# Four adjacency chunks issued first, weights on GpSimd's queue, and row sums turned by transposes, in a four-layer graph network

## The chip, the cores and the metric

The kernel runs on one core of one Trainium2 chip. The metric is the device time of a run in microseconds. A core has five engines: TensorE (PE, with its weight loads shown apart as PEld), VectorE (DVE), ScalarE (ACT), GpSimd (POOL) and SyncE (SP). SP, ACT and POOL issue DMA transfers here.

## The reference

The input is x (2708 nodes by 128 features) and a matrix adj (2708 by 2708, float32). Four graph layers follow each other, each on a normalised copy of x and each added to x. Cut to what matters here:

```python
def _lap_mul(A, x):                       # layer 0, used twice
    d = 1.0 / jnp.sqrt(jnp.sum(A, axis=-1))
    return d[:, None] * (A @ (d[:, None] * x))

h = jnp.maximum(_layernorm(x), 0.0)
z = leaky_relu(_lap_mul(adj, h) @ W1 + b1, 0.1)
S = exp(-distance(z, z) / 2), with all but the 4 largest of each row set to 0
x = x + _lap_mul(S + adj, h) @ W2 + b2
...
x = x + attention_layer(relu(layernorm(x)), adj)          # layer 1
x = x + h @ W_self + (adj @ h / max(rowsum(adj), 1)) @ W_neigh   # layer 2
x = x + relu((adj @ h) @ kernel + bias)                    # layer 3
```

The row sums of adj (the degrees) are needed before the first product with adj can be made, because its other factor is h scaled by one over their root.

## The kernel before, in words

adj goes in transposed, so a row of what the kernel loads is a column of adj. It is cut into T = 22 chunks of 128 rows (the last has 20), each 128 by 2708 float32, or 1354 KB. A chunk is used in six column blocks, KBS, five of 512 and one of 148 columns. The nodes are kept as 22 tiles of 128, in six GROUPS of four.

`chunk(i)` (line 242 for its load) issues a chunk's load on SP's queue. The last five chunks of the first pass have places of their own (`res`); the others share the pool `big` of four buffers, so the load of chunk i + 4 waits until the work on chunk i is done. The completion of loads issued by SP and ACT is counted on eight semaphores that are handed out in turn; a load whose semaphore is still in use waits for the load that uses it. POOL's loads have eight others.

The start, in program order:

- Constants (the identity by POOL), then the loads of x (lines 85 and 86), of six weights (line 90), three biases (95), the attention vector (105) and the store of a constant to `order_d` (137), all on ACT's queue.
- `layernorm_relu` for the six groups (lines 171 to 181): statistics on DVE, a root on ACT, and 22 scaled rows h0 on ACT.
- The first pass over adj: for each chunk, six products with a matrix of ones (line 341) add up the row sums in two PSUM tiles, four column blocks of the first tile and two of the second lying in bands of 32 partitions. Between the chunks `weighted(g, part)` is put, one part per chunk from chunk 3 on and kept at its place in PE's order: part 0 transposes four tiles of h0 (line 309) and ACT copies them to h0T (314), part 1 multiplies by W1 (line 320, copied to y1 by ACT, line 327), part 2 by W2 (copied to hw2 by DVE).
- The sums go to SBUF (`sum_rows`), and 44 instructions of TensorE, two for each tile (22 products), multiply one row of 128 sums by a one (line 358), which puts them into columns; seven copies put these into `degs`. From it come `rdeg` and `dinv`, and y1 is scaled (line 191).
- The first aggregation (line 255), which goes over adj again from its first chunk, with `to_z` at its end.

`evacuate` (lines 149 and 151) copies from PSUM to SBUF with DVE and ACT in turn, over all its calls in the kernel; its state is one bit. After the aggregation come the distances and the four nearest nodes (lines 448 to 480), a gather of rows (524), the second aggregation, layer 1 with sorting, a table and gathers of its rows (lines 587 to 1126), and two more aggregations for layers 2 and 3. In each aggregation the products of one chunk are made for all column blocks, and the chunks kept in SBUF come last, block by block, while `done` finishes the block before.

The order of instructions on each engine is set when the program is built, by priorities and by what is marked with `pin`, which keeps it in program order.

Of the kernel before, what the change touches and what calls it, by code (L numbers as in the profile page):

```python
# [9 lines left out]
F32 = mybir.dt.float32  # L10
# [8 lines left out]
P = 128  # L19
# [6 lines left out]
def kernel(  # L26
# [18 lines left out]
    nc = tc.nc  # L45
    N, D = x.shape
    assert D == P
    T = -(-N // P)
    TAIL = N - (T - 1) * P
    KBS = [(k0, min(512, N - k0)) for k0 in range(0, N, 512)]  # L50
    NKB = len(KBS)
    GROUPS = [(t, min(t + 4, T)) for t in range(0, T, 4)]
    L0_RES = 5
    TAIL_RES = 6

    def width(t):
        return TAIL if t == T - 1 else P

    def cols(t):
        return slice(t * P, t * P + width(t))  # L60
# [7 lines left out]
    big = ctx.enter_context(tc.tile_pool(name="big", bufs=4))  # L68
    dram = ctx.enter_context(tc.tile_pool(name="dram", bufs=1, space=DRAM))
    ps_s = ctx.enter_context(tc.tile_pool(name="ps_s", bufs=2, space=PSUM))  # L70
    ps_a = ctx.enter_context(tc.tile_pool(name="ps_a", bufs=1, space=PSUM))


    ident = consts.tile([P, P], F32, name="ident")
    make_identity(nc, ident)
    ones = consts.tile([P, P], F32, name="ones")
# [10 lines left out]

    def load_w(name, w):
        t = consts.tile([P, P], F32, name=name)
        nc.scalar.dma_start(t, w)  # L90
        return t

    def load_b(name, b):
        t = consts.tile([P, P], F32, name=name)
        nc.scalar.dma_start(t, bass.AP(tensor=b.tensor, offset=b.offset, ap=[[0, P], [1, P]]))
        return t

    w1, w2 = load_w("w1", l0_w1), load_w("w2", l0_w2)
    wg = load_w("wg", l1_w)
    ws, wn = load_w("ws", l2_ws), load_w("wn", l2_wn)  # L100
    w3 = load_w("w3", l3_k)
    b1, b2, b3 = load_b("b1", l0_b1), load_b("b2", l0_b2), load_b("b3", l3_b)
    a_nat = consts.tile([P, 2], F32, name="a_nat")
    with nc.allow_non_contiguous_dma(reason="256 elements"):
        nc.scalar.dma_start(
            a_nat, bass.AP(tensor=l1_a.tensor, offset=l1_a.offset, ap=[[1, P], [P, 2]])
        )
    ident_b = consts.tile([P, P], BF16, name="ident_b")
# [24 lines left out]
    order_d = dram.tile([P * T, 2], F32, name="order_d")  # L133
    nowhere = consts.tile([P, T, 2], F32, name="nowhere")
    nc.vector.memset(nowhere[:, :, 0:1], 1e6)
    nc.vector.memset(nowhere[:, :, 1:2], -1e5)
    nc.scalar.dma_start(order_d.rearrange("(p t) c -> p t c", t=T), nowhere)

    LAST = -(-(N - (T - 1) * PER + 3) // 16) * 16
    HALF = KBS[NKB // 2][0]  # L140
# [5 lines left out]
    def evacuate(dst, src):  # L146
        turn[0] ^= 1
        if turn[0]:
            nc.vector.tensor_copy(dst, src)
        else:  # L150
            nc.scalar.copy(dst, src)

    def pin(ins):

        return tc.keep_in_program_order(ins)

    def acc(b):
        return ps_a.tile([P, 512], F32, name=f"acc{b}")

    def span(g):  # L160
        return slice(GROUPS[g][0] * P, min(GROUPS[g][1] * P, N))
# [36 lines left out]
    def inv_sqrt(name, v):  # L198
        r = small.tile([P, T], F32, name=name + "_s")
        nc.scalar.activation(r, v, AF.Sqrt)  # L200
        d = keep.tile([P, T], F32, name=name)
        nc.vector.reciprocal(d, r)
        return d
# [25 lines left out]
        for t in range(t0, t1):  # L229
            use(t, p[: width(t), t - t0, :])  # L230

    resident = {}
    pools = {}

    def chunk(i):
        if i in resident:
            return resident[i]
        if i >= T - pools["n"]:
            c = resident[i] = pools["res"].tile([P, N + 1], F32, name=f"res{i}")
        else:  # L240
            c = big.tile([P, N + 1], F32, name="chunk", tag="big")
        pin(nc.sync.dma_start(c[: width(i), :N], adjT[i * P : i * P + width(i), :]))
        return c

    def aggregate(y, done, more=None, kept=0):

        out = [acc(b) for b in range(NKB)]
        last = T - pools["n"]  # L250

        def product(i, b):
            k0, n = KBS[b]
            w = width(i)
            nc.tensor.matmul(  # L255
                out[b][:, :n],
                y[:w, i, :],
                chunk(i)[:w, k0 : k0 + n],
                start=(i == 0),
                stop=(i == T - 1),  # L260
            )

        for i in range(last):
            if more is not None:
                more(i)
            resident[i] = chunk(i)
            for b in range(NKB):
                product(i, b)
            if i < last - kept:
                del resident[i]  # L270
            if i % 2 and last + i // 2 < T:
                chunk(last + i // 2)
        if more is not None:
            for i in range(last, T):
                more(i)
        for b in range(NKB):
            for i in range(last, T):
                product(i, b)
            if b:
                done(b - 1, out)  # L280
        done(NKB - 1, out)

    NG = len(GROUPS)
    degs = keep.tile([P, T], F32, name="degs")
    nc.vector.memset(degs, 1.0)


    rows_open = ExitStack()
    res_rows = rows_open.enter_context(tc.tile_pool(name="rows", bufs=1))
    pools.update(res=res_rows, n=L0_RES)  # L290
    l0 = ExitStack()
    res = l0.enter_context(tc.tile_pool(name="l0_res", bufs=1))

# [9 lines left out]
    def weighted(g, part):  # L303
        t0, t1 = GROUPS[g]
        if part == 0:
            p = acc(g % 2)
            for t in range(t0, t1):
                o = (t - t0) * P
                mm = nc.tensor.transpose(
                    p[:, o : o + width(t)], h0[: width(t), t, :], ident[: width(t), : width(t)]  # L310
                )
                if t == t0:
                    pin(mm)
            nc.scalar.copy(h0T[:, span(g)], p[:, : span(g).stop - span(g).start])
            return
        dst, w = ((y1, w1), (hw2, w2))[part - 1]
        p = acc(2 * part + g % 2)
        for t in range(t0, t1):
            o = (t - t0) * P
            mm = nc.tensor.matmul(  # L320
                p[: width(t), o : o + P], h0T[:, cols(t)], w, start=True, stop=True
            )
            if t == t0:
                pin(mm)
        for a, e, n in ((t0, min(t1, T - 1), P), (max(t0, T - 1), t1, TAIL)):
            if a < e:
                (nc.scalar.copy, nc.vector.tensor_copy)[part - 1](
                    dst[:n, a:e, :],
                    p[:n, (a - t0) * P : (e - t0) * P].rearrange("p (t f) -> p t f", f=P),
                )  # L330
# [3 lines left out]
    for i in range(T):  # L334
        c = chunk(i)
        w = width(i)
        if 3 <= i < 3 + 3 * NG:
            weighted((i - 3) // 3, i % 3)
        for b, (k0, n) in enumerate(KBS):
            g = 32 * (b % 4)  # L340
            nc.tensor.matmul(
                sums[b // 4][g : g + 32, :n],
                ones[:w, :32],
                c[:w, k0 : k0 + n],
                start=(i == 0),
                stop=(i == T - 1),
            )
    sum_rows = lay.tile([P, 1024], F32, name="sum_rows", tag="U")
    for half, p0, p1 in ((0, 0, 128), (1, 0, 32 * (NKB - 5)), (1, 32 * (NKB - 5), 32 * (NKB - 4))):
        n = KBS[4 * half + p0 // 32][1]  # L350
        evacuate(sum_rows[p0:p1, 512 * half : 512 * half + n], sums[half][p0:p1, :n])

    pd = [acc(j) for j in range(4)]
    for b, (t0, t1) in enumerate(GROUPS):
        j = b % 4
        for t in range(t0, t1):
            o = 512 * (b // 4) + P * (t % 4)
            nc.tensor.matmul(
                pd[j][: width(t), t : t + 1],
                sum_rows[32 * j : 32 * j + 1, o : o + width(t)],  # L360
                ones[32 * j : 32 * j + 1, :1],
                start=True,
                stop=True,
            )
    for b, (t0, t1) in enumerate(GROUPS):
        e = min(t1, T - 1)
        evacuate(degs[:, t0:e], pd[b % 4][:, t0:e])
    evacuate(degs[:TAIL, T - 1 :], pd[(NG - 1) % 4][:TAIL, T - 1 : T])
    dinv = inv_sqrt("dinv", degs)

    nc.gpsimd.tensor_tensor(xs, xs, b2[:, None, :].to_broadcast([P, T, D]), ALU.add)
# [53 lines left out]
    p = ps_s.tile([P, 512], F32, name="ps")  # L425
    pin(nc.tensor.transpose(p[:, :P], wg, ident))
    nc.vector.tensor_copy(wgT, p[:, :P])
    p = ps_s.tile([P, 512], F32, name="ps")
# [14 lines left out]
    for t in range(T):  # L443
        w = width(t)
# [245 lines left out]
    def rowtile(name):  # L690

        i = row_turn[0]
        row_turn[0] = (i + 1) % L0_RES
        return res_rows.tile([P, N + 1], F32, name=name, tag=f"res{T - L0_RES + i}")
# [229 lines left out]
    p = acc(0)  # L924
# [44 lines left out]
    for t0, t1 in GROUPS:  # L969
        p = acc(1 + t0 // 4 % 5)  # L970
        for t in range(t0, t1):
            o = (t - t0) * P
# [4 lines left out]
                start=True,  # L977
                stop=True,
# [3 lines left out]
        for t in range(t0, t1):  # L982
            o = (t - t0) * P
# [31 lines left out]
    for t in range(T):  # L1015
        if t + 3 < T:
            fetch(t + 3)
        o = rowtile("knots")
        for b, (k0, n) in enumerate(EKBS):
            p = acc(b)  # L1020
# [30 lines left out]
    rows, factors = {}, {}  # L1051
# [227 lines left out]
```

## Time and profile before

| | |
|---|---|
| median of 5 runs | 1318.88 us (1310.98 to 1320.64) |
| profiled execution | 1314.6 us, its span 1312.6 us |
| mean granted TensorE clock | 0.901 |
| busy, share of the span | PE 83%, PEld 39%, DVE 43%, ACT 31%, POOL 17% |
| chain that ended last | PE 57%, DMA 17%, DVE 10%, issue 9% |
| DMA | 297 MB, 227 GB/s over the span |
| first sums of chunk 0 | at 7.50 us |
| first product of line 255 | at 95.68 us |

The span is the time from the first to the last instruction. A row of a timeline gives the start, the busy time, the engine, the line, the operation with its tiles, how many there were, and in brackets how long the engine was idle before and what ended that. The rows of a wait view give who waited for whom, the total, how often, and the longest. The rows of a DMA view give a queue's packets, megabytes, and the time of its packets as a share of the 16 DMA engines; q1 is SP's queue, q10 ACT's and q0 POOL's. The granted clock is 1.00 at full speed.

### The profile page before, as it was taken

To read this page: it belongs to the slowest core of one execution; us is meant where nothing else is said; L and a number is where in the kernel's file an instruction comes from. 1 tells how busy PE (TensorE), PEld (TensorE's weight loads), DVE (VectorE), ACT (ScalarE), POOL (GpSimd) and SP (SyncE) were. 2 spreads that over 40 slices of the span, in tenths; PEclk is the share of its full clock that TensorE was granted. 3 is DMA by queue.
4 is the path that set the end of the run, shared out by engine and by line. 5 is a ranking of instruction groups with operands and counts; after the bars stand their busy time and mean duration, and the time that the engine had idled before them with its cause. 6 is when DMAs were issued, how large, how long until landed. Compare 5 with 4: busy or idle time off the path is not lost.

```text
span 1312.6 us, 10207 instructions
## 1 busy us (share of the span) xinstructions
PE 1090.9 (83%) x3637; PEld 514.6 (39%) x3637; DVE 564.1 (43%) x1172; ACT 408.2 (31%) x643; POOL 227.6 (17%) x188
## 2 busy tenths in 40 slices
PE   4879999999683369897776871587889999999998
PEld 1334444444231124464433430233344445545444
DVE  2020026999822001783455763899970031113003
ACT  3100014444400000475666743677840021003000
POOL 0100000000077710034111102576400000000000
PEclk8989999999795579887899986888889999999999
DMA  8997800000463351256799997999949926752831
GB/s 318 424 384 257 292 1 1 0 1 0 171 265 96 94 225 81 87 229 234 213 390 394 368 381 306 422 422 412 354 161 420 352 78 227 267 184 81 302 125 43
DMA packets 39506, 297.31 MB, mean 227 GB/s; under 512 B 6749, under 2 KB 10680, under 8 KB 13116
## 3 DMA queue, kind: packets, MB, share of 16 engines
q1 hardware_dynamic: 23806, 201.04, 40.1%
q0 software_dynamic: 13216, 93.62, 19.0%
q10 hardware_dynamic: 2434, 2.01, 0.6%
q8 instruction: 29, 0.48, 0.1%
q14 instruction: 21, 0.17, 0.0%
HBM read 264.46 MB, written 32.87 MB: 227 GB/s over the span
## 4 chain that ended last, share of the span: by engine, by line
PE 57%; DMA 17%; DVE 10%; issue 9%; another core or an unknown queue 6%; POOL 1%; ACT 1%; SPq 0%; POOLq 0%; DVEq 0%; ACTq 0%
PE acc L255 37%; DMA mov<-in_adj_dram,src_u 8%; PE acc L448 8%; DVE hi L1116 3%; DMA chunk<-in_adj_dram 3%; DVE hi L1104 3%; DMA hi<-table,hi_u 2%; PE acc L454 2%; PE acc L1021 2%; DMA res<-in_adj_dram 2%; PE ps L224 1%; PE acc L1126 1%; DMA xs<-in_x_dram 1%; PE ps L222 1%
## 5 line engine op out<-in xcount | busy, mean ns | idle before, releaser
L255 PE MATMUL acc<-chunk,y 128*128 128x512 f32 (+1 forms) x408 | 178.5, 588 | 73.0 <-issue 55.7
L1126 PE MATMUL acc<-hi,xw 128*128 128x512 f32 (+2 forms) x264 | 119.5, 613 | 60.8 <-DVE hi L1116 60.8
L524 POOL DMA_INDIRECT gath<-ydr,near_u x88 | 83.2, 946 | 408.4 <-DMA ydr<-y 322.1
L255 PE MATMUL acc<-chunk,h 128*128 128x512 f32 (+1 forms) x384 | 148.0, 542 | 0.0
L255 PEld LDWEIGHTS acc<-chunk,y 128*128 128x128 f32 x408 | 78.9, 203 | 172.6 <-issue 158.3
L1021 PE MATMUL acc<-mov,wt 128*128 128x512 f32 (+1 forms) x264 | 114.9, 588 | 35.2 <-DMA mov<-in_adj_dram,src_u 32.7
L448 PE MATMUL acc<-zT 128*128 128x512 f32 (+2 forms) x264 | 107.7, 552 | 0.0
L1126 PEld LDWEIGHTS acc<-hi,xw 128*128 128x128 f32 (+1 forms) x264 | 53.7, 212 | 126.6 <-DVE hi L1116 63.7
L1025 DVE COPY mov<-acc 2x512 f32<-2x512 f32 (+1 forms) x126 | 74.3, 611 | 60.0 <-PE acc L1021 58.3
L255 PEld LDWEIGHTS acc<-chunk,h 128*128 128x128 f32 x384 | 68.8, 190 | 74.1 <-issue 74.1
L1021 PEld LDWEIGHTS acc<-mov,wt 128*128 128x128 f32 x264 | 51.0, 204 | 95.3 <-issue 78.8
L457 ACT COPY strip<-acc 128x512 f32<-128x512 f32 (+2 forms) x132 | 60.5, 559 | 71.4 <-issue 58.5
L255 PE MATMUL acc<-chunk,attended 128*128 128x512 f32 x192 | 73.8, 547 | 0.0
L1058 POOL DMA_INDIRECT lo<-table,lo_u x22 | 56.9, 2585 | 76.3 <-DVE hi L1104 35.3
L448 PEld LDWEIGHTS acc<-zT 128*128 128x128 f32 (+1 forms) x264 | 46.6, 186 | 56.3 <-issue 35.5
L1026 ACT COPY knots<-acc 128x512 f32<-128x512 f32 x88 | 50.2, 585 | 57.2 <-DVE mov L1025 36.5
L1104 DVE SCALAR_TENSOR_TENSOR hi<-lo,lam,hi 128x2708 f32<-128x2708 f32 (+4 forms) x25 | 67.2, 2697 | 1.0
L1116 DVE SCALAR_TENSOR_TENSOR hi<-row_all,inv_s,hi 128x2708 f32<-128x2708 f32 (+4 forms) x25 | 67.0, 2692 | 0.0
L1108 ACT ACTIVATE hi<-hi,lam 128x2708 f32<-128x2708 f32 (+4 forms) x25 | 56.7, 2280 | 32.9 <-issue 23.8
L459 DVE MAX8 top_v<-strip 128x8 f32<-128x2708 f32 (+1 forms) x22 | 64.7, 2966 | 0.5 <-ACT strip L457 0.4
L461 DVE FIND_INDEX8 top_i<-top_v,strip 128x8 uint32<-128x2708 f32 x20 | 59.2, 2974 | 0.0
L255 PE MATMUL acc<-res,h 128*128 128x512 f32 (+1 forms) x144 | 58.9, 551 | 0.0
(267 smaller groups left out, 1162.4 us busy)
## 6 DMA issues: line engine op xcount, KB each, us to landing
chunk<-in_adj_dram SPq DMA_DIRECT2D x110, 1354.0 KB
table<-knots SPq DMA_DIRECT2D x20, 1354.5 KB
res<-in_adj_dram SPq DMA_DIRECT2D x9, 1354.0 KB
ydr<-y SPq DMA_DIRECT2D x2, 704.0 KB
gath<-ydr,near_u POOLq DMA_INDIRECT x88
chunkY<-in_adj_dram SPq DMA_DIRECT2D x1, 1354.0 KB
chunkU<-in_adj_dram SPq DMA_DIRECT2D x1, 1354.0 KB
table<-knots SPq DMA_DIRECT2D x1, 1333.3 KB
```

The lines of the kernel that those rows point to most:

```text
L255: nc.tensor.matmul(out[b][:, :n], y[:w, i, :], chunk(i)[:w, k0 : k0 + n], start=(i == 0), stop=(i == T - 1),)
L448: mm = nc.tensor.matmul(zz[b][:w, :n], zT[:, cols(t)], zT[:, k0 : k0 + n], start=True, stop=False)
L457: nc.scalar.copy(s[:w, k0 : k0 + n], zz[b][:w, :n])
L459: nc.vector.max(top_v[:w, t, :], s[:w, :])
L461: nc.vector.max_index(top_i[:w, t, :], top_v[:w, t, :], s[:w, :])
L524: nc.gpsimd.indirect_dma_start(out=g[:w, :], out_offset=None, in_=ydr[:, :], in_offset=bass.IndirectOffsetOnAxis(ap=near_u[:w, t, k : k + ...
L1021: nc.tensor.matmul(p[:, :n], wt[:, t, :], moving[t][:, k0 : k0 + n], start=True, stop=True)
L1025: nc.vector.tensor_copy(moving[t + 1][:2, k0 : k0 + n], p[:2, :n])
L1058: nc.gpsimd.indirect_dma_start(out=dst[:w, :], out_offset=None, in_=table[:, :], in_offset=bass.IndirectOffsetOnAxis(ap=idx[:w, t : t + 1] ...
L1104: nc.vector.scalar_tensor_tensor(num, lo[:w, c], kap, num, op0=ALU.mult, op1=ALU.add)
L1116: nc.vector.scalar_tensor_tensor(att[:w, c], row_all[:w, c], inv_s[:w, t : t + 1], att[:w, c], op0=ALU.max, op1=ALU.mult,)
L1126: nc.tensor.matmul(py[b][:, :n], xw[:w, t, :], att[:w, k0 : k0 + n], start=(t == 0), stop=(t == T - 1),)
```

## The change

It has two parts. The first four chunks are loaded by calls at the head of the kernel, ahead of the constants, and used when the first pass comes to them; the weights, biases and other small loads move from ACT's queue to POOL's; `weighted` starts at chunk 4 instead of 3. And the row sums are turned into columns by ten transposes, with four copies by DVE, in place of the 22 products and seven calls of `evacuate`. `pin`, `chunk` and the pool `rows` are defined earlier for it, unchanged.

```diff
+    rows_open = ExitStack()
+    res_rows = rows_open.enter_context(tc.tile_pool(name="rows", bufs=1))
+    pools.update(res=res_rows, n=L0_RES)
+    FIRST = 4
+    for i in range(FIRST):
+        resident[i] = chunk(i)
...
     def load_w(name, w):
         t = consts.tile([P, P], F32, name=name)
-        nc.scalar.dma_start(t, w)
+        nc.gpsimd.dma_start(t, w)
         return t
...
-        nc.scalar.dma_start(t, bass.AP(tensor=b.tensor, offset=b.offset, ap=[[0, P], [1, P]]))
+        nc.gpsimd.dma_start(t, bass.AP(tensor=b.tensor, offset=b.offset, ap=[[0, P], [1, P]]))
...
-        nc.scalar.dma_start(
+        nc.gpsimd.dma_start(
             a_nat, bass.AP(tensor=l1_a.tensor, offset=l1_a.offset, ap=[[1, P], [P, 2]])
         )
...
-    nc.scalar.dma_start(order_d.rearrange("(p t) c -> p t c", t=T), nowhere)
+    nc.gpsimd.dma_start(order_d.rearrange("(p t) c -> p t c", t=T), nowhere)
...
-        if 3 <= i < 3 + 3 * NG:
-            weighted((i - 3) // 3, i % 3)
+        if i >= FIRST and i < FIRST + 3 * NG:
+            weighted((i - FIRST) // 3, (i - FIRST) % 3)
...
+        if i < FIRST:
+            del resident[i]
...
-    pd = [acc(j) for j in range(4)]
-    for b, (t0, t1) in enumerate(GROUPS):
-        j = b % 4
-        for t in range(t0, t1):
-            o = 512 * (b // 4) + P * (t % 4)
-            nc.tensor.matmul(
-                pd[j][: width(t), t : t + 1],
-                sum_rows[32 * j : 32 * j + 1, o : o + width(t)],
-                ones[32 * j : 32 * j + 1, :1],
-                start=True,
-                stop=True,
-            )
-    for b, (t0, t1) in enumerate(GROUPS):
-        e = min(t1, T - 1)
-        evacuate(degs[:, t0:e], pd[b % 4][:, t0:e])
-    evacuate(degs[:TAIL, T - 1 :], pd[(NG - 1) % 4][:TAIL, T - 1 : T])
+    for g0, g1 in [(0, 4)] + [(b, b + 1) for b in range(4, NKB)]:
+        pd = acc(max(g0 - 3, 0))
+        r0, r1 = 32 * (g0 % 4), 32 * (g0 % 4 + g1 - g0)
+        e = min(4 * g1, T)
+        for c in range(min(4, e - 4 * g0)):
+            w = min(width(4 * b + c) for b in range(g0, g1))
+            o = 512 * (g0 // 4) + P * c
+            nc.tensor.transpose(
+                pd[:w, P * c : P * c + r1 - r0], sum_rows[r0:r1, o : o + w], ident[r0:r1, r0:r1]
+            )
+        pv = pd.rearrange("p (c g r) -> p g c r", c=4, g=4)[:, : g1 - g0, :, 0]
+        m = min(e, T - 1) - 4 * g0
+        nc.vector.tensor_copy(
+            degs[:, 4 * g0 : 4 * g0 + m].rearrange("p (g c) -> p g c", g=g1 - g0),
+            pv[:, :, : m // (g1 - g0)],
+        )
+        if e == T:
+            nc.vector.tensor_copy(degs[:TAIL, T - 1 :], pd[:TAIL, P * m : P * m + 1])
```

In the built program SP's order is chunks 0 to 3, then chunk 4 (after chunk 0's sums), 5, and 6, which waits for chunk 2's sums and for the semaphore that x's load uses. ACT's order has the two loads of x, the table load, all 22 scaled rows, and then the first copy to h0T. POOL's order has one weight load between the two instructions that make the identity, and the others after them.

More of the change, by code (lines that the diff above doesn't have):

```diff
@@ L71, with pin, chunk @@
     ps_a = ctx.enter_context(tc.tile_pool(name="ps_a", bufs=1, space=PSUM))
+    def pin(ins):
+        return tc.keep_in_program_order(ins)
+    resident = {}
+    pools = {}
+    def chunk(i):
+        if i in resident:
+            return resident[i]
+        if i >= T - pools["n"]:
+            c = resident[i] = pools["res"].tile([P, N + 1], F32, name=f"res{i}")
+        else:
+            c = big.tile([P, N + 1], F32, name="chunk", tag="big")
+        pin(nc.sync.dma_start(c[: width(i), :N], adjT[i * P : i * P + width(i), :]))
+        return c
+    rows_open = ExitStack()
[4 more added lines that the diff above has]
+        resident[i] = chunk(i)
     ident = consts.tile([P, P], F32, name="ident")
@@ L151, in evacuate @@
             nc.scalar.copy(dst, src)
-    def pin(ins):
-        return tc.keep_in_program_order(ins)
     def acc(b):
@@ L230, in node_product @@
             use(t, p[: width(t), t - t0, :])
[L232 to L243, printed above, removed]
     def aggregate(y, done, more=None, kept=0):
@@ L285 @@
     nc.vector.memset(degs, 1.0)
-    rows_open = ExitStack()
-    res_rows = rows_open.enter_context(tc.tile_pool(name="rows", bufs=1))
-    pools.update(res=res_rows, n=L0_RES)
     l0 = ExitStack()
```

## The prediction

> **What bounds the kernel now.** I read the page's chain first: PE has 57% of it and DMA 17%, spread over stages, so a change at the start is worth what it takes off the stretch up to the first product of the first aggregation (line 255). The timeline of that stretch, rows of several engines:
>
> ```profile
> 7.50 3.59 PE L341 MATMUL ps<-chunk,ones 128*32 128x512 f32 x12 [7.50 <-DMA chunk<-in_adj_dram]
> ...
> 15.14 0.49 DVE L171 BATCH_NORM_STATS2 ln_st<-xs 128x6 f32<-128x128 f32 x2 [13.26 <-DMA xs<-in_x_dram]
> ...
> 20.71 3.19 ACT L181 ACTIVATE h<-xs,ln_nm,ln_rs 128x128 f32<-128x128 f32 x8 [0.26 <-DVE ln_nm L176]
> ...
> 27.50 2.98 PE L341 MATMUL ps<-chunk,ones 128*32 128x512 f32 x12 [2.00 <-DMA chunk<-in_adj_dram]
> ...
> 28.46 2.42 ACT L181 ACTIVATE h<-xs,ln_nm,ln_rs 128x128 f32<-128x128 f32 x6
> ...
> 30.41 1.71 PE L320 MATMUL acc<-w,h0T 128*128 128x128 f32 x8
> ...
> 47.44 1.90 PE L341 MATMUL ps<-chunk,ones 128*32 128x512 f32 x12 [0.76 <-DMA chunk<-in_adj_dram]
> ...
> 84.85 3.73 PE L341 MATMUL ps<-res,ones 128*32 128x512 f32 x24 [1.68 <-DMA res<-in_adj_dram]
> ...
> 88.56 4.94 PE L358 MATMUL acc<-ones,sum_rows 1*128 1x1 f32 x44
> ...
> 95.68 16.80 PE L255 MATMUL acc<-chunk,y 128*128 128x512 f32 x38 [2.17 <-DVE y L191]
> ```
>
> The row sums wait for adj from chunk 4 or so to chunk 20 (47.44 is chunk 9, 84.85 chunk 20), one chunk per 3.25 to 3.3 us. From 95.7 on PE runs without a pause for 100 us. So the stretch is a load, a tail of 88.58 to 95.65, and what is lost in front. The loss is in the first 22 us. The waits of the load queue, and then the DMA queues from 5 to 10 us and from 10 to 15 us (packets, MB, share):
>
> ```profile
> SPq L242 <- DMA w<-in_L_gnn_W_dram: 13.6, 1, 13.6
> ```
> ```profile
> q1 hardware_dynamic: 171, 1.67, 82.2%
> q10 hardware_dynamic: 163, 0.33, 17.2%
> ```
> ```profile
> q10 hardware_dynamic: 1115, 1.31, 96.3%
> q1 hardware_dynamic: 18, 0.03, 1.8%
> ```
>
> Two chunks are issued at 0.8 to 1.7 us. The third (15.34) waits 13.6 us on a weight load with whose completion its semaphore is shared. The second pair is the row that decides my forecast: while adj (q1) has work, x (q10) gets one packet of 2 KB for each of adj's, 0.33 MB in 5 us; as soon as adj runs dry, x takes all 16 engines, and lands at 15.14.
>
> **The change, part by part.**
>
> *Chunks 2 and 3 at once.* That ends the waits at 13.6 us and after. But it takes from x the stretch in which it ran alone. The built program issues four chunks, chunk 4 when chunk 0's sums are done (7.5 + 3.6 = 11.1), chunk 5 at about 13.6; chunk 6 waits for the semaphore that x's load uses. So x shares the engines with six chunks. Two ways to its landing: at 0.066 MB/us (the row above) its 21 x 128 x 512 B = 1.38 MB take 20.8 us from the first packet at 5.3, that is 26.1, and the weights' packets and 0.6 us to the semaphore come on top. Or by the sum: six chunks of 1.387 MB, x and 0.6 MB of weights are 10.3 MB; at 400 GB/s (the mean of that view) 25.7 us, from 2.0, plus 0.6: 28.3. Since everything in the queues must be done by then whatever the order, 28.3 is also an upper end. The lower is 24 (x starting 2 us earlier). I take 28.3, 13.2 us later than now.
>
> The Trainium skill, "DMA: Bandwidth & Descriptors", Queues, rings and completion order, says that an engine drains a whole packet of some 9 to 17 descriptors from one queue before it turns to the next. The row shows 9.8 KB, one row of adj, per turn, so the turns here are shorter; by the rule x would get almost nothing until chunk 5 is through, and its landing would still be 28.3, since that is a sum of bytes.
>
> *Layernorm.* ACT loses the eleven issues that held it until 18.64 and its table load after them. In the built program the first scaled rows come after eight statistics pairs at 0.26, a cast, five more statistics at 0.2, two reciprocals and two factors: 4.2 us after x (5.57 now). From the first to the last of the 22 rows ACT takes 10.17 now (20.71 to 30.88), with a copy of 0.56 in it that partly hides; I take 10.1. So they end at 28.3 + 14.3 = 42.6. The copy h0T, which now stands ahead of the last six rows, stands behind all of them in the new order: 43.2. PE, in program order, has the first transposes ahead of chunk 4 (one chunk later than now): 28.3 + 4.2 + 1.6 = 34.1, 0.65 for them, then chunk 4's sums at half clock, 3.6 as at 7.50: 38.4. The first product w1 needs h0T: 43.2, 1.64 (30.41 to 32.05 now), then chunk 5's sums as at 27.50, 2.98: 47.8.
>
> *Four buffers.* Queued behind these PE waits are the releases: chunk 8 goes out at 38.4 and chunk 9 at 47.8. A chunk on an idle queue takes 1.1 us to its first packet (issue at 102.57), 3.3 of transfer and 0.4: chunk 9 lands at 52.6, where it now starts at 47.44: +5.2. PE needs 2.73 a chunk from there (1.90 + 0.83), DMA 3.3, so the rest is load-bound as now and keeps the +5.2. This is the stall that takes the place of the one removed. The last product group now falls between chunks 20 and 21, both landed: +0.8.
>
> *Weights by POOL.* Eleven issues; POOL's gathers take 946 ns each (the group at line 524), so some 10 us, ending near 12. Needed are w1 at 43 and b2 for line 371, which waits for the rows anyway; the identity comes one issue later, needed at 34. Cover: 30 us; without it 1 us per issue. I take nothing. The same page, in Issuing engine by pattern, puts a simple load on SP and calls GpSimd's path the slower one (about 1 us against 0.6 to the first byte); by that the weights would come an estimated 0.4 us later each, under the same cover.
>
> *Ten transposes.* 44 products of one row take 4.94 us, and the degree copies end at 94.01. Instead: the first copy of sums (0.69) as now, four transposes 0.65 (the row of four at line 309), a copy of 0.2, the copy of 148 columns (0.30), the last transposes 0.25 and two copies of 0.16: degrees ready 1.75 us after the last sum where it is 5.4 now. The 1.64 us from there to the first product stay: 3.4 instead of 7.07, -3.65. Bounds: at half clock throughout the transposes cost 0.9 more (-2.75); if the copies overlap fully, -4.2.
>
> *Clock.* The granted clock is 0.50 from 90 to 99.6, so the first 4 us of line 255 run at half: 2.1 us lost. With a shorter pause it may or may not drop: between -2.1 and +1; I take -0.5, nearest to the row as it stands.
>
> *Evacuations.* Seven calls fewer turn the alternation of ACT and DVE round in all later stages (0.57 against 0.69 us for a copy). The two alternate per group, so it is nearly even; -1 to +1, taken as 0.
>
> **Sum.** +5.2 + 0.8 - 3.65 - 0.5 = +1.85 us on the profiled execution: its span of 1312.6 lies in a run of 1314.6, so 1316.5. That run is 4.3 under the median of 1318.88, to which I add the same: 1320.7. About 0.5% (6.6 us) is what a measurement of this kernel can tell from no change, so this is "same". With the bounds (x at 24: -4.3; tail and clock +0.9, +1.5; copies 1) the likeliest case alone runs from 1313 to 1324.
>
> **The rivals.**
>
> *x is not held back (faster).* If x keeps its landing near 15 to 18 us, no PE wait comes, and the load streams throughout: 29.3 + 1.4 + 0.6 = 31.3 MB at 420 GB/s are 74.5 us from 2.0, plus the 1 us that chunk 20 now takes over the usual: 77.5 where it is 84.85, -7.3; with +0.8, -3.65 and -0.5 the sum is -10.7, 1308.2. For it: 11 to 22 us now moves well under 400 GB/s. Against: the 163 against 171 packets. It begins to win over the present load when x lands before 23.
>
> *PE stays cold (slower).* Place: chunks 5 to 9, after two PE pauses of 12 and 5 us. At half clock a chunk takes 3.6 + 1.5 = 5.1 us, over the 3.3 of the load, so each cold chunk from chunk 6 on delays the buffer, and so the load, by 1.8. One or two cold chunks are the 2.98 already in the sum; three bring +5.4, 1326; four 1328. For it: the clock was 0.50 again from 29 to 31 us, right after work had begun at 27.5. Against: from 32 on it was full at 60% duty. The Trainium skill, "TensorE: Matmul & The Clock Gate", Part 1, puts the warm-up at about 3.4 us of sustained work; by that one chunk would be cold and nothing is added, an estimate; the rows of 28 to 32 us are less kind.
>
> *The change does not do what it says.* The first chunk is issued at 0.82 us now, so "ahead of everything" moves only chunks 2 and 3; if x also stays as it is held now, only the transposes are left with their clock, -4.15 and 1314.7, within the same band.
>
> **How the numbers follow.** My case with the last rival has 0.50, faster 0.23, cold PE 0.27. Faster reaches over 0.5% nearly always; cold PE from three chunks on, most of its chance, and my case's edges give 0.04 to slower and 0.01 to faster: 0.24, 0.45, 0.31. The range takes in both rivals: 1307 to 1329.
>
> **What would show it.** Right: statistics (line 192) start near 28, h0T's copy near 43, chunk 9's sums near 52.6, the last sum near 94.6, the first product of line 255 some 3.4 us after it; POOL's issues done by 15. Wrong: statistics before 23, no PE wait on ACT before 45, or granted clock at 0.50 after 48. It would be wrong altogether if stages after 100 us differ in length by over 2 us.

## The result, and the profile after

The changed kernel takes 1324.75 us (median of 42 runs, 1316.35 to 1330.78) where the kernel before takes 1318.46 (79 runs, 1310.55 to 1326.11): ratio 1.0044, 95% interval 1.0032 to 1.0056, or 4.2 to 7.4 us more. The median is under the 0.5% which the prediction set as the bound (the interval reaches 0.56%), but the interval excludes zero, and the loss is larger than the 1.85 us that were worked out. The profiled execution took 1323.66 us with a span of 1321.6 and a mean granted clock of 0.894.

The rows of the changed kernel's timeline that answer to those of the prediction (start, busy time, engine, line, operation, and in brackets the idle time before it and what ended it). Line 192 is the statistics, 202 the scaled rows, 314 the transposes of h0, 319 the copy h0T, 325 the weighted products, 346 the row sums, 368 the ten transposes, 263 the first aggregation:

```profile
30.04 0.49 DVE L192 BATCH_NORM_STATS2 ln_st<-xs 128x6 f32<-128x128 f32 x2 [28.17 <-DMA xs<-in_x_dram]
...
33.73 3.19 ACT L202 ACTIVATE h<-xs,ln_nm,ln_rs 128x128 f32<-128x128 f32 x8 [1.03 <-DVE ln_nm L197]
...
34.36 1.54 PE L314 MATMUL acc<-ident,h 128*128 128x128 f32 x4 [7.11 <-ACT h L202]
...
35.83 3.62 PE L346 MATMUL ps<-chunk,ones 128*32 128x512 f32 x12
...
41.35 2.42 ACT L202 ACTIVATE h<-xs,ln_nm,ln_rs 128x128 f32<-128x128 f32 x6 [0.25 <-DVE ln_nm L197]
...
43.68 0.56 ACT L319 COPY h0T<-acc 128x512 f32<-128x512 f32 x1
...
44.29 2.08 PE L325 MATMUL acc<-w,h0T 128*128 128x128 f32 x8 [4.84 <-ACT h0T L319]
46.30 2.47 PE L346 MATMUL ps<-chunk,ones 128*32 128x512 f32 x12
```
```profile
92.62 1.90 PE L346 MATMUL ps<-res,ones 128*32 128x512 f32 x12 [1.66 <-DMA res<-in_adj_dram]
...
97.08 1.53 PE L368 MATMUL acc<-ident,sum_rows 128*128 128x128 f32 x10
...
100.38 11.87 PE L263 MATMUL acc<-chunk,y 128*128 128x512 f32 x24 [1.77 <-DVE y L212]
```

Read from the top: x lands at 30.0 where it landed at 15.1. PE waits 7.11 us for the first scaled rows, and 4.84 us more for h0T, because ACT makes all 22 rows (33.73 to 43.77) before it turns to the copy. Chunk 20's sums stand at 92.62 (84.85 before). From the last sum to the first product of line 263 it is 3.3 us where it was 7.1. The bottom two rows are the gain, everything above is the loss, and the loss is the larger: the first product starts 4.7 us later.

The waits of the load queue up to 100 us (total, times, longest) show how PE's two waits reach the load. Before, buffers that PE had not released held the queue for 20.4 us, at most 3.1 at a time; now it is 41.3, at most 8.9. The row before, then two rows of the changed kernel:

```profile
SPq L242 <- PE ps L341: 20.4, 10, 3.1
```
```profile
SPq L87 <- PE ps L346: 41.3, 11, 8.9
...
SPq L87 <- DMA xs<-in_x_dram: 13.4, 2, 13.2
```

In the table by stretches (busy time of PE, PEld, DVE, ACT and POOL, each with its count, then granted clock, DMA share, GB/s) the load falls off while PE waits and then works cold (at half the clock):

```profile
35.00:40.00 5.00, 4.45 (x15) 0.93 (x14) 1.88 (x16) 4.75 (x14) 0.00 (x0) 0.50 0.62 259
40.00:45.00 5.00, 0.71 (x3) 0.71 (x4) 0.57 (x4) 3.98 (x11) 1.14 (x1) 0.50 0.79 277
45.00:50.00 5.00, 5.00 (x31) 2.69 (x34) 0.10 (x1) 0.58 (x1) 5.00 (x1) 0.75 0.15 29
```

SP's queue moved nothing from 39.0 to 40.4 and from 45.2 to 49.8. Before, it had one such gap, 11.1 to 16.3. The change traded one gap of 5.2 us for two of 6.0 together, and a load that is slower in front, which the DMA queues from 5 to 10 us show (packets, MB, share):

```profile
q1 hardware_dynamic: 147, 1.42, 73.4%
q10 hardware_dynamic: 130, 0.27, 14.0%
q0 software_dynamic: 116, 0.26, 13.8%
```

x (q10) still gets about one packet for each of adj's (q1), but POOL's queue (q0) now takes its turns too.

### The profile page after: what moved, and what is told of

Read it like the earlier page. It is cut to its first block, busy times and chain, and to the rows that moved or that the text cites. A ratio compares the mean times of both kernels' runs of the same rounds, so it can differ in the third digit from the quotient of the medians.

```text
span 1321.6 us, 10139 instructions
## 1 busy us (share of the span) xinstructions
PE 1096.1 (83%) x3603; PEld 515.0 (39%) x3603; DVE 560.9 (42%) x1173; ACT 410.0 (31%) x639; POOL 235.6 (18%) x199
## 4 chain that ended last, share of the span: by engine, by line
PE 58%; DMA 16%; DVE 11%; issue 10%; POOL 3%; ACT 1%; SPq 0%; another core or an unknown queue 0%; POOLq 0%; DVEq 0%; ACTq 0%
PE acc L263 37%; DMA mov<-in_adj_dram,src_u 8%; PE acc L458 8%; DVE hi L1126 4%; DVE hi L1114 4%; DMA hi<-table,hi_u 2%; DMA xs<-in_x_dram 2%; PE acc L464 2%; POOL gath L534 2%; PE ps L842 2%; DMA res<-in_adj_dram 2%; PE ps L346 1%; PE ps L245 1%; PE acc L1136 1%; PE ps L243 1%
```

## The experiments

The theory under test: small loads off ACT's queue let chunks 2 to 5 go out at once; x, which shares the engines with them packet by packet, lands 15 us later; ACT's 22 rows and then the copy h0T follow; PE, in program order, waits; four buffers are not released; the load queue idles. Against it stood the rivals that the load is late by bytes alone, that the place of the issues matters, and that a cold PE is the cost.

The runs were on three chips. On the first the kernel before takes 1318 us, on the others 1230, so each ratio is to the kernel before on the same chip; in the first 100 us, in which the change works, the changed kernel's profiles from two of them agree within 0.3 us.

| run | statistics start | h0T copied | ten (or 44) start | first product | ratio to before, 95% |
|---|---|---|---|---|---|
| before | 15.14 | 28.55 | 88.56 | 95.68 | 1 |
| turn_only | 14.88 | 28.37 | 90.41 | 93.80 | 0.9959 [0.9938, 0.998] |
| weights_only | 30.29 | 41.82 | 97.70 | 103.45 | 1.0088 [1.0065, 1.0112] |
| load_only | 30.40 | 44.60 | 98.81 | 105.21 | 1.0079 [1.0055, 1.0104] |
| after | 30.04 | 44.24 | 97.08 | 100.38 | 1.0044 [1.0032, 1.0056] |
| x_first | 8.67 | 28.51 | 89.15 | 92.53 | 0.9969 [0.9952, 0.9987] |
| copy_early | 30.23 | 37.58 | 91.20 | 94.50 | 0.998 [0.9954, 1.0006] |
| x_fifth | 26.49 | 34.47 | 87.97 | 91.27 | 0.9953 [0.9927, 0.9979] |
| x_first_act | 9.06 | 27.82 | 87.30 | 90.59 | 0.9934 [0.9906, 0.9962] |
| x_first_act3 | 8.74 | 25.09 | 85.60 | 88.98 | 0.9925 [0.9901, 0.995] |
| after_again | 30.14 | 44.35 | 97.20 | 100.51 | 1.0034 [1.0019, 1.005] |
| copy_early_again | 30.37 | 37.71 | 91.40 | 94.70 | 0.9978 [0.9962, 0.9994] |
| small_late | 26.42 | 40.62 | 94.19 | 97.56 | 0.998 [0.9966, 0.9994] |
| x_first_again | 8.62 | 28.31 | 86.28 | 89.59 | 0.9952 [0.9934, 0.997] |

Rows from turn_only to x_first are of one chip (with the kernel before's profile), the next four of another, the last four of the third.

**The turn alone: turn_only.** The kernel before, with only this part of the change:

```diff
-    pd = [acc(j) for j in range(4)]
-    for b, (t0, t1) in enumerate(GROUPS):
...
+    for g0, g1 in [(0, 4)] + [(b, b + 1) for b in range(4, NKB)]:
...
+            nc.tensor.transpose(
```

> Before, with the ten transposes alone; loads and queues as before. Theory (x held back by the chunks issued ahead of it costs the load, the transposes give back a part): the last row sum stays near 88.6 us, the first product of the first aggregation comes 3.3 us after it instead of 7.1, near 91.9, and the run is 3.8 us shorter, ratio 0.997. Rival (the turned alternation of ACT and DVE in the later evacuations costs the time): the first product comes as early, but the gain is gone at the end, ratio 1.000 or more.

Measured: 0.9959 [0.9938, 0.998], 2.6 to 8.2 us less. The two rows of its timeline:

```profile
90.41 1.62 PE L360 MATMUL acc<-ident,sum_rows 128*128 128x128 f32 x10
...
93.80 2.90 PE L255 MATMUL acc<-chunk,y 128*128 128x512 f32 x3 [1.76 <-issue]
```

3.4 us between them for 7.1: the tail is worth the 3.7 that the prediction gave it, and the change's gain is this part. Some 1.4 of the 3.7 hang on the clock: in weights_only below, where it was 1.00 from 97 to 100 us, the 44 instructions and what follows them took 5.75 us, in the kernel before 7.1 at 0.50 from 90 on. (In this execution the ten start 1.9 us later than the 44 in the profile of the kernel before, so the first product is only 1.9 earlier: chunk 20's sums start 0.5 later, and the last two chunks' sums took 5.1 us for 3.7, with the clock at 0.50 from 86 to 88 us.)

**The load alone: load_only.** The changed kernel with the 44 instructions of the kernel before, and their seven copies, put back (the same lines, turned round).

> After, with the 22 products of before in place of the ten transposes. Theory: statistics at 30 us and the last row sum at 97.1 as in after, the first product 7.1 later, at 104.2: 8.5 us longer than before, ratio 1.0065. Rival (evacuations turned round): the alternation is here as in before again, so the run would be near before, ratio 1.001 or less.

Measured: 1.0079 [1.0055, 1.0104], 7.3 to 13.7 us more. The parts add up: -0.0041 and +0.0079 make +0.0038, and the whole change measured +0.0044.

**The weights' queue alone: weights_only.** The kernel before, with its small loads issued by POOL; no load is moved to the head of the program:

```diff
-        nc.scalar.dma_start(t, w)
+        nc.gpsimd.dma_start(t, w)
...
-    nc.scalar.dma_start(order_d.rearrange("(p t) c -> p t c", t=T), nowhere)
+    nc.gpsimd.dma_start(order_d.rearrange("(p t) c -> p t c", t=T), nowhere)
```

> Before, with only the eleven small loads moved from ACT's to POOL's queue: no loads at the head, products from chunk 3 on as before. Theory: what held chunks 2 and 3 back was the weights' semaphores, so they go out in the first 2.5 us here too, x is starved as in after (statistics near 30 us), PE waits for x ahead of chunk 3 instead of 4, the last row sum comes near 96.5 and the run is some 8 us longer, ratio 1.006. Rival (the calls at the head of the kernel do it, the weights' queue does not matter): statistics near 15 us, ratio 1.000 or a little less.

Measured: 1.0088 [1.0065, 1.0112]. SP issues its first four chunks at 0.82, 1.27, 1.73 and 2.2 us, as in the changed kernel, without any call having been moved; x lands as late, and PE waits:

```profile
34.62 1.54 PE L309 MATMUL acc<-ident,h 128*128 128x128 f32 x4 [11.64 <-ACT h L181]
...
41.88 1.16 PE L320 MATMUL acc<-w,h0T 128*128 128x128 f32 x8 [2.17 <-ACT h0T L314]
```

So the calls "ahead of everything" are not what starves x: taking the small loads off ACT's queue does it alone, since they shared the completion semaphores that held chunk 2 back. The rival of the place of the calls falls.

**x first: x_first and x_first_again.** The changed kernel, with x's main load on SP's queue ahead of the four chunks:

```diff
+    xs = keep.tile([P, T, D], F32, name="xs")
+    pin(nc.sync.dma_start(xs[:, : T - 1, :], x[: (T - 1) * P, :].rearrange("(t p) f -> p t f", p=P)))
...
-    nc.scalar.dma_start(xs[:, : T - 1, :], x[: (T - 1) * P, :].rearrange("(t p) f -> p t f", p=P))
```

> After, with the load of x's first 21 tiles issued on SP's queue ahead of the four chunks instead of on ACT's beside them. Theory: x lands near 8 us, no PE wait for the scaled rows or h0T comes after chunk 3, the load streams at 3.3 us a chunk, the last row sum comes near 82 us, the first product near 85.5: 10 us shorter than before, ratio 0.992. Rival (the small loads on POOL's queue are what costs the load): statistics early, but the last row sum still after 88, ratio 0.997 or more.

Measured: 0.9969 [0.9952, 0.9987]. The direction is the theory's, and no wait of PE on ACT is left, but the size was put too high. Part of the rest is in front: with x in packets of 2 KB and POOL's loads beside it, the stream ran at 331 GB/s from 5 to 10 us and 353 from 10 to 15, and chunk 0's sums start only at 13.4; chunk 19 came 2.3 us earlier than in the kernel before, where streaming from the start had been expected to bring more. Another part is at the end: after a wait of 2.3 us for chunk 20 the clock was 0.50 from 84 to 86 us, and from chunk 20's sums to the ten it took 6.05 us, in x_first_again 4.45.

> The changed kernel with x's main load on SP's queue ahead of the four chunks, a second time, beside the changed kernel and on rounds shared with it. Theory: ratio 0.007 to 0.008 below that of the changed kernel, as the first time (0.9969 for 1.0044). In the run with the small loads back on ScalarE the ratio was 0.9934 under the higher clock: if the third queue costs nothing once x is first, this run comes to the same where the clock is the same, and to 0.997 where it is low.

Measured, beside the changed kernel at 1.0034: 0.9952 [0.9934, 0.997], 0.0082 below it as expected.

**x fifth: x_fifth.** The same line, but behind the four chunks.

> The changed kernel with x's main load issued on SP's queue behind the four chunks, not on ScalarE's beside them. x is then no longer sharing the engines row by row, but stands behind 5.6 MB. Theory (x's landing sets PE's wait and the buffers): 5.6 MB and 1.4 MB at the 350 to 400 GB/s of this stretch land at 18.5 to 22, the statistics start there, near 20 for 30.04, the first weighted products near 34 for 44.29, both gaps of the load queue are gone, and the last sum ends near 92, ratio 0.998 to 1.000. It should lie between the run with x first (0.997) and the changed kernel (1.0044). Rival (only x ahead of all chunks helps, since the four chunks are consumed no sooner): ratio 1.004.

Measured: 0.9953 [0.9927, 0.9979]. The time was better than expected and the landing worse: the statistics start at 26.5, not at 20, since x's 672 packets of 2 KB took 114 ns each in the mean, 4.8 us on 16 engines, behind chunks whose last packet came at 21.5. What made it fast was not foreseen in the text: in this build the copy h0T stands ahead of the second eight rows on ACT, and ends at 34.5. Beside small_late below, on another chip, whose x lands at the same moment (26.4) but whose copy ends at 40.6, that is a comparison for free: the copy 6.1 us earlier, the first product 6.3 us earlier.

**The copy early: copy_early and copy_early_again.** The changed kernel with ACT's order alone changed; x stays late:

```diff
-    for g in range(NG):
-        layernorm_relu(h0, g)
+    layernorm_relu(h0, 0)
+    layernorm_relu(h0, 1)
     for i in range(T):
...
-            nc.scalar.copy(h0T[:, span(g)], p[:, : span(g).stop - span(g).start])
-            return
+            return nc.scalar.copy(h0T[:, span(g)], p[:, : span(g).stop - span(g).start])
...
-            weighted((i - FIRST) // 3, (i - FIRST) % 3)
+            copy = weighted((i - FIRST) // 3, (i - FIRST) % 3)
+            if i == FIRST:
+                with tc.issue_after(copy.ins):
+                    for g in range(2, NG):
+                        layernorm_relu(h0, g)
```

> The changed kernel with one thing moved: the layer norm rows of groups 2 to 5 stand on ScalarE behind the copy of h0T for group 0, where the changed kernel has all 22 scaled rows ahead of that copy (43.68 us). The loads, their queues and PE's order are those of the changed kernel, so x lands as late as there (statistics near 30). Theory (the late x costs the time through ScalarE's order, PE's wait and the buffers that are not released): h0T's copy near 37, no wait of PE behind chunk 4's sums (4.84 us before), chunk 5's sums end near 43.5 for 48.77, chunk 9 is issued there for 48.82, the load's second gap (45.21 to 49.75) goes while the first (39.0 to 40.4) stays, the last sum ends near 92.5 for 97.08, and the ratio to the kernel before is 1.001 for 1.0044. Rival (the load is late by its bytes and by x's packets alone, so the wait on PE costs nothing): last sum at 97, ratio 1.004.

Measured: 0.998 [0.9954, 1.0006].

> The changed kernel with the layer norm rows of groups 2 to 5 behind the copy of h0T for group 0 on ScalarE, beside the changed kernel. Its last sum ended 4.5 us earlier than the changed kernel's (by the run before this one), so theory: ratio 0.0035 below that of the changed kernel in these same rounds. Rival (the wait of PE is made good by the load afterwards): within 0.001 of it.

Measured: 0.9978 [0.9962, 0.9994], beside 1.0034 [1.0019, 1.005] for the changed kernel in the same rounds. From PE's and ACT's rows of the second run:

```profile
34.69 1.54 PE L314 MATMUL acc<-ident,h 128*128 128x128 f32 x4 [8.68 <-ACT h L202]
36.16 3.62 PE L349 MATMUL ps<-chunk,ones 128*32 128x512 f32 x12
39.71 1.37 PE L324 MATMUL acc<-w,h0T 128*128 128x128 f32 x8
41.01 1.90 PE L349 MATMUL ps<-chunk,ones 128*32 128x512 f32 x12
```
```profile
37.15 0.56 ACT L319 COPY h0T<-acc 128x512 f32<-128x512 f32 x1
```

x is as late as ever, but the second wait is gone, chunk 5's sums end at 42.9 for 48.8, chunk 9 is issued at 42.96 for 48.83, and the load's second gap is gone while the first (39.3 to 40.8) stays. The last sum comes 5.8 us earlier than the changed kernel's, 1.3 more than the 4.5 expected (the first copy_early had already shown 5.9, 91.20 for 97.08): without the pause PE runs its products in 1.37 us where after_again has 2.07, and the next sums in 1.90 instead of 2.38. The ratio is 0.0056 under the changed kernel's, 6.9 us, of which the first pass shows 5.8. The rival that the load makes the wait good afterwards falls, and an order on ACT alone more than undoes the loss.

**The small loads later: small_late.** The changed kernel with POOL's transfers held until x has landed:

```diff
+    seen = consts.tile([P, 1], F32, name="seen")
+    landed = nc.gpsimd.tensor_copy(seen, xs[:, 0, 0:1])
+    with tc.issue_after(landed.ins):
+        w1, w2 = load_w("w1", l0_w1), load_w("w2", l0_w2)
...
```

> The changed kernel with GpSimd's eleven small transfers issued only after x's rows have landed (a one-column read of x stands ahead of them on GpSimd). x then shares the engines with SP's chunks alone. This measures the term that the prediction set at 1.5 us, GpSimd's small packets in front of x. Theory (144 packets of 4 KB at 173 ns over each of 16 engines' share come to 2.9 us, and they sit ahead of x): statistics at 27 to 27.5 for 30.0, h0T's copy near 41, chunk 9 near 46, last sum near 94.5, ratio 1.002. Rival 1 (x is held only by the one-for-one turns with the chunks' rows, so the small transfers merely change places with chunk rows): statistics at 29.5 to 30, ratio 1.004. Rival 2 (the weights land too late for the first products): a wait of PE for the weights behind 44, ratio 1.005 or more.

Measured: 0.998 [0.9966, 0.9994]. The queues from 10 to 15 us:

```profile
q1 hardware_dynamic: 177, 1.59, 82.5%
q10 hardware_dynamic: 178, 0.36, 18.8%
```

Statistics at 26.42 for 30.14: POOL's small loads ahead of x cost it 3.7 us, rival 1 falls, and rival 2 too (PE waits for h0T, not for weights). The first pass moved as the theory said (chunk 9 issued at 45.4, last sum at 94.2, 3.0 us earlier). The ratio moved by 0.0054, some 6.6 us; where the other 3.6 us come from is open. In the profiles the distance of the two kernels stays near 3.0 until 550 us, swings between 3 and 7 from 590 to 700, is near 7.4 to 870 and 8.9 from 900 on; no run tells why.

**x first without the third queue: x_first_act, and from chunk 3: x_first_act3.** The small loads go back to ACT behind x's tail; in the second, `weighted` starts at chunk 3 again:

```diff
-        if i >= FIRST and i < FIRST + 3 * NG:
-            weighted((i - FIRST) // 3, (i - FIRST) % 3)
+        if 3 <= i < 3 + 3 * NG:
+            weighted((i - 3) // 3, i % 3)
```

> The run with x first on SP's queue, but the ten small loads back on ScalarE's queue as in the kernel before, in place of GpSimd's. Tells the price of the third queue when x is not behind it. Theory (GpSimd's 4 KB packets took 173 ns each and held the engines for 2.9 us in all, where 512 byte packets of ScalarE's queue held them for 2.3 us; the first 20 us of the run with x first moved only 300 to 350 GB/s): the stream gains at most 1.5 us at chunk 19, ratio 0.996 for 0.997. Rival 1 (no difference between the queues once x is out of the way): 0.997. Rival 2 (the eight shared completion semaphores hold chunk loads back behind the small loads again, as in the kernel before): chunk 2 issued after 10 us, ratio over 0.999.

Measured: 0.9934 [0.9906, 0.9962]. Its interval covers that of x_first_again in part, so once x is first no price of the third queue is shown. Chunk 19's sums start 0.4 us earlier than in x_first_again (76.94 for 77.34), where at most 1.5 were expected. The first product (90.59) is 1.0 us later than there, but that is the clock, 0.55 from 82 to 84 us and 0.60 from 84 to 86. Chunk 1 waits 4.6 us for a weight load and goes out at 9.5 us, chunk 2 at 9.8, so the shared semaphores hold chunks back again; but PE has x by then, and the queue does not run empty.

> The same as the run with x first and the small loads on ScalarE's queue, with the weighted products starting at chunk 3, as in the kernel before, for chunk 4: the last group of products then stands behind chunk 19 and no longer between chunks 20 and 21, where it delayed the last sums. Theory: the last sum ends 0.5 to 0.8 us earlier than with the start at chunk 4, ratio lower by 0.0005. Rival (x lands early enough for chunk 4 only, so that PE waits at chunk 3): the last sum at the same time or later, no gain.

Measured: 0.9925 [0.9901, 0.995], with the last sum 1.7 us earlier than in x_first_act (expected 0.5 to 0.8). Of that the group of products moved away from the last sums is 0.7, as expected; chunk 20's sums start 0.6 later, and some 1.5 are the clock, which stayed at 1.00 here until 86 us. The medians differ by 3.2 us, the intervals overlap, so only the profile speaks for this last step. It is the best of all, 0.75% under the kernel before on its chip.

**The changed kernel again: after_again.**

> The changed kernel itself once more, beside three others that are compared with it, because the granted clock of the run with the copy of h0T early was higher (0.928) than that of the first runs (0.894), and its ratio of 0.998 stands without the changed kernel's beside it. Theory (the delay in the first pass is a matter of the load's order and does not hang on the clock of later stages): ratio 1.004 as before, statistics near 30, last sum near 97. Rival (where the clock is higher, the cold first products cost less and the change is worth more): ratio below 1.001.

Measured: 1.0034 [1.0019, 1.005], statistics at 30.14, the last sum at 97.2: the same delay where the clock is higher. The rival falls.

## Why the prediction was right, and where its steps were off

The call of "no change by the bound" and the range hold; the mechanism that was named (x held back, PE waiting in program order, buffers not released, load-bound from there, given back in part by the transposes) is what the runs show. But the loss was put at 1.85 us and is 6.3 by the medians (4.2 to 7.4), and 4.7 already at the first product. The terms, on the profiled executions:

| term | predicted | measured |
|---|---|---|
| x, statistics start | 28.3 | 30.04 |
| rows end, h0T copied | 42.6, 43.2 | 43.77, 44.24 |
| chunk 5's sums end, chunk 9 issued | 47.8 | 48.77, 48.82 |
| stream from chunk 9 on | +5.2 | +7.8 |
| last product group | +0.8 | +0.7 |
| tail | -3.65 | -3.8 |
| clock at the start of line 263 | -0.5 | +0.5 |
| sum, in the first aggregation | +1.85 | +5.2 |

*Chunks 2 and 3 at once* was mis-sized in one place: "28.3 is also an upper end". It was a sum of bytes at 400 GB/s, and the rate was the wrong part of it. From 1.8 us to chunk 5's last packet in after_again (31.3) the 10.3 MB moved at 349 GB/s; in small_late, without POOL's packets, the same chunks and x (9.7 MB) were through at 27.6, which is 376. POOL's 144 packets of 4 KB took 320 ns each in the mean (173 in the median, which the expectations of x_first_act and small_late give beside the same 2.9 us), 46 us together or 2.9 on 16 engines for 0.59 MB that the sum had at 1.5, and the two kernels' x is 3.7 us apart. An upper end needs the slowest rate that the mix can have, not a mean of one view.

*Four buffers* lost 2.6 us in three small steps. Chunk 9 was issued 1.0 later, the late x less what went quicker on the way. From issue to its last packet it took 5.1 us (48.82 to 53.92) for the 4.4 that were summed up. And the prediction set a landing (52.6) against a start of sums (47.44): in the kernel before chunk 9's last packet came at 46.06, so 1.4 us lie between the two, of which 0.4 was counted. Packet against packet, chunk 9 is 7.9 us later, and 7.8 stands at chunk 19. Comparing like with like would have given +6.1 from the prediction's own numbers (52.2 against 46.06).

*Ten transposes*, the *last product group* and *weights by POOL* as issues (done at 11.1, nothing waiting) held. *Layernorm* held within 0.6: the rows end 13.7 us after x where 14.3 was worked out.

*Clock* had the sign wrong: the pause is shorter, but the clock was at 0.50 again from 100 to 105 us, and from 106 us on the products of the first aggregation stand 5.2 us behind those of the kernel before, where the first stood 4.7 behind.

*PE stays cold* did not come. Chunk 4 and part of chunk 5 were cold, but that was in the sum: 3.6 us for chunk 4's sums, which took 3.62, and 4.6 for the first products and chunk 5's sums, which took 4.5 (44.29 to 48.77). The granted clock was 0.50 up to 47.4 us and 1.00 from 47.6 on, so no third cold chunk delayed a buffer. The rise came some 3.2 us after PE began again at 44.29. The Trainium skill, "TensorE: Matmul & The Clock Gate", Part 1, has a window of about 3.4 us of sustained work for that, free-running, so that the count of cold products varies; 3.2 fits, but in copy_early_again PE was busy without a pause from 34.7 and the clock stood at 0.50 until 40.2, 5.5 us, more than one window and less than two. In the changed kernel the second wait came before the clock had risen (it was 0.50 from 34.36 to 39.45 too); without it, copy_early_again is 1.2 us quicker over the same products and sums.

The other page of the Trainium skill that it weighed, "DMA: Bandwidth & Descriptors", Queues, rings and completion order, has an engine change queues after a packet, typically of 9 to 17 descriptors. The runs show a change after each packet, and small packets: x's 672 packets of 2 KB, four of its rows each, alternate with single rows of a chunk (10.8 KB), in the changed kernel (130 against 147) and in small_late (178 against 177). Counted in rows, the turns are shorter than the page's, as the prediction had read from its own lines.

The prediction's last sign of being wrong altogether, stages after 100 us that differ in length by over 2 us, did appear in the profiles, but the runs do not lay it on the change. Between matching instructions the shift is 5.0 to 5.4 us up to 400, 8 to 11 from 425 to 475, 6.3 from 475 to 550, swings between 3.7 and 8.3 from 550 to 800, is 6.2 or 6.3 to 950, and 9.0 from 975 on. The jump of 2.8 falls where the changed kernel's granted clock was 0.50 and 0.64 in the two stretches of 5 us at the start of an aggregation (0.50 and 0.95 in the kernel before). A jump of 2.8 to 4.5 us at the same place separates the kernel before's profile from those of turn_only, load_only, weights_only and x_first as well, so it points to that one execution; the medians, 6.3 apart, do not carry it. load_only, which has the alternation of the kernel before, drifts in the later stages too, so the seven calls of `evacuate` are not needed to explain it.

*The change does not do what it says* was right about the head of the program: chunks 2 and 3 were held by a semaphore, not by their place. *x is not held back* was the prize that the change missed: x first brings 0.9925 to 0.997.

## What to carry to other kernels

A load that is freed takes its turns from whatever else is in the queues; before a bulk stream is let go, put the small load on which the in-order engine depends ahead of it, on the same queue if need be. When a wait shows up behind a late input, look at what the engine that makes the input does first: here one copy put ahead of fourteen rows took back 5.8 us, with x still 15 us late. And compare a landing with a landing: 1 us of the miss was a landing set against a start.

## What the runs showed of the hardware

Loads by POOL's queue went in 144 packets of 4 KB, 173 ns in the median and 320 in the mean, 46 us of packet time in all; by ACT's queue the same loads and x's last rows went in 1172 packets of 512 B, 27 and 29 ns in the median, 32 and 47 in the mean, 37 us in the kernel before and 55 in turn_only. Small as they are, POOL's loads kept x back by 3.7 us, where their bytes had been counted at 1.5.

Two chips ran the same program 7% faster than the first. In the changed kernel's two profiles the difference, 80 us, arises between 391 and 482 us, in the second aggregation beside the gathers of rows: on the slower chip most of PE's products there start 2.1 to 3.5 us apart with "issue" named as what ended the idle time, on the other they run back to back. No run here tells why. Two rows of the slower chip, then the row of the other chip that the stretch begins in:

```profile
467.06 1.01 PE L263 MATMUL acc<-chunk,y 128*128 128x512 f32 x1 [1.79 <-issue]
469.86 1.01 PE L263 MATMUL acc<-chunk,y 128*128 128x512 f32 x1 [1.79 <-issue]
```
```profile
364.50 36.08 PE L263 MATMUL acc<-chunk,y 128*128 128x512 f32 x95
```
